# Layer 3's context projections: from layer 1's attention to layer 0's experts

## The chip, the cores and the metric

The kernel runs on one core of a Trainium2 chip. A core has TensorE (PE below; its weight loads are listed as PEld), VectorE (DVE), ScalarE (ACT), GpSimd (POOL) and SyncE (SP), which issues most of the direct DMA transfers; indirect gathers are issued by POOL. The metric is the device time of one execution in microseconds (us), compared by the median of several runs. The profile is one execution, with times counted from the start of its span.

## The reference

The reference is a decoder of four layers on x of shape (8, 256, 256), with a context of shape (8, 120, 192) that no layer changes. Each layer adds an attention, an attention to the context and a feed-forward network, each followed by a layer norm. Cut to what matters here:

```python
# layer 0, feed-forward: 8 experts, every token goes to the best one
expert_idx = jnp.argmax(router_probs, axis=-1)
for e in range(8):
    h = gelu(x_flat @ w1[e] + b1[e], approximate=False)   # 256 -> 1024
    out += where(expert_idx == e, expert_w, 0)[:, None] * (h @ w2[e] + b2[e])

# layer 1, attention to the context: 16 heads of 16
q = x @ w_q + b_q;  k = context @ w_k + b_k;  v = context @ w_v + b_v
out = softmax(q k^T / 4) v @ w_o + b_o

# layer 3, attention to the context: 8 heads of 64
k = context @ Wk      # (8, 120, 192) @ (192, 512)
v = context @ Wv      # (8, 120, 192) @ (192, 512)
```

The last two products hang on nothing that the layers compute, so a kernel may do them at any time before layer 3.

## The kernel before

The stages run in this order: layer 0's attention, its attention to the context (`l0_xattn`, about 206 to 254 us), its experts (`l0_ffn`, about 254 to 512, the end running into the next stage), layer 1's attention (`l1_attn`, to 756), its attention to the context (`l1_xattn`, to about 925), its experts, and the rest. Tokens are held as 16 tiles of 128 (`X`), and turned as `xT`. While a stage runs, the weights of the next one are loaded into the other of two buffers (`load`, L120): a stage's buffer is free for the stage after the next once its last reader is done.

Inside a stage the program names the engine of each operation, and the framework puts the operations of each engine in an order of its own: by place in the program, but what is ready may go ahead of what is not. It also places the semaphores. Once built, each engine's order is fixed. PSUM has eight banks; two belong to transposes (`ps_t`) through the whole kernel, and each stage opens pools for the others.

**Layer 0's experts** (L1016 to L1122) have four parts. Routing: 16 pairs of matmuls give the logits `plog`, then DVE finds the best expert per token (`route`, L891), PE counts places (`pos`, `cnt`), DVE works out the slot of each token, PE finds for each slot its token (`found`, in `takers`, L951), and ACT and DVE make the list `take` of it. Three PSUM banks serve this, then one. The blocks: 23 blocks of 128 slots (L1093 to L1113); each gathers its expert's weights where they differ from those in the buffer (`we`, two buffers), its 128 rows (`xe`), and does 256 to 1024, Gelu on ACT, and back to 256, with four PSUM banks (`ph`, `py`). DVE adds the bias and SP stores the block (`yd`, L1113). The taking back (L1114 to L1122): POOL gathers each token's row of `yd`, DVE scales and adds it and does the norm, PE transposes it into `xT`.

**Layer 1's attention to the context** goes by batches b = 0 to 7 in `attention16` (L640). For each b the program has the scores for the exponentials of b (`exps16`), in two steps, between them the scores of b + 1 that give the largest per row (`largest16`, reduced by DVE at L509), then transposes of these into q (`lower16`, L544, added by DVE at L546), the sums of values (`sums16`, L613), and for even b the projections of the next pair (`project`, L739). What follows a batch (the projection out, the norm, the transposes, the router's logits of the next stage in `choose`, L755) is put into the next batch. All of these take their PSUM banks in turn from one ring of eight (`bank`, L455).

The work that is moved is `context3` (L770). For one batch it projects layer 3's keys (four 128-row parts of two products each) and values (two products 512 wide), has ACT copy the keys (L777) and DVE the values (L782) out of PSUM, and SP store both in DRAM (L778, L783). `inside` (L785) puts it behind the second step of scores of each batch, ahead of `lower16`. The stored values have 65 columns per head, and the last is 1; two buffers (`v3`) get it once from POOL (L736). Layer 3 reads keys and values back at L1758 and L1760, from 1537 us on. The two weights come with layer 1's (L721 to L724) into the buffer that layer 0's experts used for their gate, so they are issued once the last router matmul has read it.

Of the kernel before, what the change touches and what calls it, by code (L numbers as in the profile page):

```python
# [11 lines left out]
F32 = mybir.dt.float32  # L12
# [6 lines left out]
PSUM = bass.MemoryType.PSUM  # L19

P = 128
B, S, D = 8, 256, 256
NT = B * S // P
NTOK = B * S
SC, DC = 120, 192
# [20 lines left out]
class Net:  # L46
# [672 lines left out]
    def load_l1_xattn(self):  # L719

        *w, spare = self.load(  # L721
            *((f"l1x_w{n}", 2) for n in "qkvo"), ("l3x_wk", 2), ("l3x_wv", 2),
            rows=("l1x_bv", "l1x_bo"), spare=16 * NT + 8,
        )  # L724
        top = spare[:, : 16 * NT].rearrange("p (a t k) -> p a t k", a=2, k=8)
        self.top1, self.top1_i, self.w_sums = top[:, 0], top[:, 1].bitcast(U32), spare[:, 16 * NT :]
        return w

    def l1_xattn(self, w):
        nc = self.nc  # L730
        wq, wk, wv, wo, wk3, wv3, bv, bo = w
        with ExitStack() as ctx:
            work, low, vps = self.attn16_pools(ctx, "x1", SC, 1)
            v3 = [work.tile([SC, 8, 65], F32, name=f"v3{n}", bufs=1) for n in range(2)]
            for t in v3:
                nc.gpsimd.memset(t[:, :, 64:], 1.0)  # L736
            bv, bo = self.everywhere(bv, work, "bv"), self.everywhere(bo, work, "bo")

            def project(b, vp):  # L739
                kv = work.tile([P, 2, 2, 2 * SC], F32, name="kv")  # L740
                ctxT = self.ctxT[:, :, b * SC : (b + 2) * SC]
                self.project16(kv, wk, ctxT, self.col("l1x_bk"), 2 * SC, "k")
                qv = work.tile([P, 2, 2, 512], F32, name="qv")
                self.project16(qv, wq, self.xT[:, :, b * S : (b + 2) * S], self.col("l1x_bq"), 512, "q")
                for n in range(2):
                    pv = self.bank([P, 512])[:SC, :D]
                    self.mm(pv, [(ctxT[:, c, n * SC : (n + 1) * SC], wv[:, c, :]) for c in range(2)])
                    self.values16(vp[:, n, 0, :], pv, SC, bv)
                return qv, kv

            zero = work.tile([1, D], F32, name="zero", bufs=1)
            nc.gpsimd.memset(zero, 0.0)
            nc.sync.dma_start(self.xd1[0:1, :], zero)

            def choose(b):  # L755

                xd = self.xd1[1 + b * S : 1 + (b + 1) * S, :].rearrange("(t p) d -> p t d", p=P)
                nc.sync.dma_start(xd, self.X[:, 2 * b : 2 * b + 2, :])
                pl = self.bank([P, 2, 256])[:, :, :32]
                for j in range(2):  # L760
                    i = 2 * b + j
                    self.mm(pl[:, j, :], [(self.xT4[:, c, i, :], self.gate1[:, c, :]) for c in range(2)])
                lg = work.tile([P, 2, 32], F32, name="lg")
                nc.scalar.copy(lg, pl)
                for j in range(2):
                    i = 2 * b + j
                    nc.vector.max(self.top1[:, i, :], lg[:, j, :])
                    nc.vector.max_index(self.top1_i[:, i, :], self.top1[:, i, :], lg[:, j, :])

            def context3(b):  # L770

                ctxT = self.ctxT[:, :, b * SC : (b + 1) * SC]
                pk = self.bank([P, 4, P])[:, :, :SC]
                for m in range(4):
                    self.mm(pk[:, m, :], [(wk3[:, c, m * P : (m + 1) * P], ctxT[:, c, :]) for c in range(2)])
                kT = work.tile([P, 4, SC], F32, name="k3")
                nc.scalar.copy(kT, pk)  # L777
                nc.sync.dma_start(self.k3[b], kT.rearrange("p m s -> p (m s)"))  # L778
                pv = self.bank([P, 512])
                self.mm(pv[:SC], [(ctxT[:, c, :], wv3[:, c, :]) for c in range(2)])  # L780
                v = v3[b % 2]
                nc.vector.tensor_copy(v[:, :, :64], pv[:SC].rearrange("p (h d) -> p h d", d=64))  # L782
                nc.sync.dma_start(self.v3[b], v.rearrange("p h d -> p (h d)"))  # L783

            def inside(b):  # L785
                return lambda: None, lambda: context3(b), lambda: None

            self.attention16(
                project, low, vps, [SC], False, wo, bo, work, then=choose,
                ready=(lambda: None, lambda: None, inside),  # L790
            )

            o = 0
            for j, (_, k, n, _) in enumerate(L2X):
                n *= k // P
# [215 lines left out]


    def load_l0_ffn(self):
        return self.load(("l0f_gate", 2))

    def l0_ffn(self, w):  # L1016
        nc, tc = self.nc, self.tc
        (gate,) = w
        E, FC = 8, 8
        NB = NT + E - 1  # L1020
        with (
            tc.tile_pool(name="f0", bufs=1) as pool,
            tc.tile_pool(name="f0w", bufs=3) as work,
            tc.tile_pool(name="f0d", bufs=1, space=bass.MemoryType.DRAM) as dram,
        ):
            with tc.tile_pool(name="f0r", bufs=1, space=PSUM) as ps:
                plog = ps.tile([P, NT, E], F32, name="plog")
                for i in range(NT):
# [34 lines left out]
            )  # L1063
            with tc.tile_pool(name="f0t", bufs=1, space=PSUM) as ps:
                take = self.takers(block[:, 1], group, 1, pool, work, ps, pool)
            past = pool.tile([P, NB, E], F32, name="past")
            nc.vector.tensor_tensor(
                past,
# [20 lines left out]
            with tc.tile_pool(name="f0p", bufs=2, space=PSUM) as ps:  # L1089
                for turn, n in enumerate(turns):  # L1090
# [20 lines left out]
                    y = work.tile([P, D], F32, name="y")  # L1111
                    nc.vector.tensor_tensor(y, py, b2, ALU.add)  # L1112
                    nc.sync.dma_start(yd[n * P : (n + 1) * P, :], y)  # L1113
                for i in range(0, NT, 2):  # L1114
                    z = work.tile([P, 2, D], F32, name="z")
                    for j in range(2):
# [1260 lines left out]
```

## Time and profile before

| | |
|---|---|
| median of 9 runs | 2445.3 us (2441.64 to 2452.65) |
| profiled execution | 2450.77 us, span 2448.9 us |
| busy share of the span | PE 83%, PEld 61%, DVE 63%, ACT 38%, POOL 28% |
| mean granted clock of PE | 0.90 |
| `l0_xattn`, 206 to 254 us | PE busy 42.1 of 48 us |
| routing, 254 to 293 us | PE busy 22.1 of 39 us, granted clock 0.50 |
| expert blocks, 293 to 492 us | PE busy 183.7 of 199 us |
| taking back until layer 1 starts, 492 to 512 us | PE busy 2.6 of 20 us |
| `l1_attn`, 512 to 756 us | PE busy 223.9 of 244 us |
| `l1_xattn`, 756 to 925 us | PE busy 149.9 of 169 us, DVE 119.2, ACT 69.8 |

A line of the order of time has the start in us, the time in us from start to end, the engine, the line of the program, the operation, what it writes and from what, shapes, and how many were merged; in brackets the idle time of the engine before it and what ended that. Matmuls are pipelined, so their durations overlap, and of a run of them the start of the next line is the better end. A product in float32 is issued as two instructions, so `context3` shows as 16 matmuls of 120 columns and 4 of 512. A window's line has its length, the busy time of each engine in it, the granted clock as a share of full speed, the busy share of the DMA engines and GB/s.

### The profile page before, as it was taken

To read this page: it belongs to the slowest core of one execution; us is meant where nothing else is said; L and a number is where in the kernel's file an instruction comes from. 1 tells how busy PE (TensorE), PEld (TensorE's weight loads), DVE (VectorE), ACT (ScalarE), POOL (GpSimd) and SP (SyncE) were. 2 spreads that over 40 slices of the span, in tenths; PEclk is the share of its full clock that TensorE was granted. 3 is DMA by queue.
4 is the path that set the end of the run, shared out by engine and by line. 5 is a ranking of instruction groups with operands and counts; after the bars stand their busy time and mean duration, and the time that the engine had idled before them with its cause. 6 is when DMAs were issued, how large, how long until landed. Compare 5 with 4: busy or idle time off the path is not lost. (4 is left out here: it accounts for less than half of the span.)

```text
span 2448.9 us, 38544 instructions
## 1 busy us (share of the span) xinstructions
PE 2023.4 (83%) x14051; PEld 1483.5 (61%) x14051; DVE 1545.1 (63%) x5022; ACT 931.0 (38%) x2056; POOL 682.9 (28%) x731
## 2 busy tenths in 40 slices
PE   7998699969998986987779777578898899877895
PEld 4665588835556665863445443466677778665674
DVE  4666300076666766664567688678678877853774
ACT  2332133313333345221334225234554455443662
POOL 1012222031112112544341102344345334520232
PEclk9999699979999996996899888788999999887997
DMA  2000443210002111861110100222222122310000
GB/s 92 2 2 18 164 149 119 74 37 1 2 1 78 48 41 63 255 201 58 35 36 2 65 1 32 85 75 60 69 62 78 49 78 69 114 49 9 1 18 19
DMA packets 69045, 147.54 MB, mean 60 GB/s; under 512 B 15864, under 2 KB 39560, under 8 KB 66928
## 3 DMA queue, kind: packets, MB, share of 16 engines
q0 software_dynamic: 30528, 81.81, 11.0%
q1 hardware_dynamic: 35564, 59.47, 7.3%
q10 hardware_dynamic: 2756, 3.72, 0.4%
q8 instruction: 113, 1.85, 0.3%
q14 instruction: 84, 0.69, 0.1%
HBM read 175.56 MB, written 23.76 MB: 81 GB/s over the span
## 5 line engine op out<-in xcount | busy, mean ns | idle before, releaser
L988 POOL DMA_INDIRECT rows<-in_l2f_table_dram,index x240 | 249.6, 1040 | 259.9 <-PE po L1661 87.3
L144 PE MATMUL ph<-xeT,we 128*128 128x128 f32 (+1 forms) x992 | 175.8, 319 | 19.0 <-DMA we<-in_l0f_experts_dram,wrow 14.1
L144 PE MATMUL pp<-xT,w 128*128 128x256 f32 (+1 forms) x672 | 186.7, 422 | 2.6 <-DVE hT L1135 1.6
L144 PEld LDWEIGHTS ph<-xeT,we 128*128 128x128 f32 x992 | 151.3, 201 | 40.8 <-DMA we<-in_l0f_experts_dram,wrow 15.4
L185 PE MATMUL pt<-ident,X 128*128 128x128 f32 x352 | 75.8, 331 | 117.3 <-DVE X L199 107.0
L600 POOL TENSOR_TENSOR aT<-sides,inv 128x256 f32<-128x256 f32 x64 | 46.6, 728 | 420.9 <-DVE sides L598 327.4
L144 PEld LDWEIGHTS pp<-xT,w 128*128 128x128 f32 x672 | 134.7, 208 | 29.1 <-issue 6.1
L186 ACT COPY xT<-pt 128x512 f32<-128x512 f32 x88 | 51.5, 585 | 256.9 <-PE pt L185 256.8
L185 PEld LDWEIGHTS pt<-ident,X 128*128 128x128 f32 x352 | 47.5, 161 | 154.4 <-DVE X L199 71.2
L988 POOL DMA_INDIRECT xe<-xd,take x87 | 86.3, 992 | 180.1 <-DVE y L1112 75.4
L1661 PE MATMUL po<-rows,diag 128*128 128x256 f32 x480 | 126.3, 403 | 11.5 <-ACT diag L1660 11.4
L1112 DVE TENSOR_TENSOR y<-py,we 128x256 f32<-128x256 f32 x23 | 9.8, 424 | 195.8 <-PE py L144 195.8
L144 PE MATMUL py<-we,hT 128*128 128x256 f32 x496 | 130.1, 387 | 0.2 <-DVE hT L1135 0.2
L564 ACT ACTIVATE e<-sc 128x512 f32<-128x512 f32 (+1 forms) x146 | 77.4, 602 | 100.4 <-PE sc L492 66.9
L1661 PEld LDWEIGHTS po<-rows,diag 128*128 128x128 f32 x480 | 92.1, 200 | 31.8 <-ACT diag L1660 19.0
L1106 ACT ACTIVATE hT<-ph,we 128x128 f32<-128x128 f32 x184 | 65.6, 366 | 117.8 <-PE ph L144 93.4
L1599 DVE SCALAR_TENSOR_TENSOR junk<-rows,X 128x256 f32<-128x256 f32 x224 | 93.8, 419 | 20.6 <-DMA rows<-in_l2f_table_dram,index 18.6
L492 PE MATMUL sc<-kv,qv 32*128 32x128 f32 (+2 forms) x1520 | 103.3, 317 | 3.0 <-ACT e L564 1.9
L144 PE MATMUL sc<-xT,w 128*128 128x512 f32 x216 | 103.4, 628 | 1.4 <-ACT xT L186 1.4
L199 DVE TENSOR_SCALAR X<-z,ln_mv,rs_y 128x256 f32<-128x256 f32 x176 | 66.4, 420 | 58.5 <-POOL rs_y L155 58.2
L492 PEld LDWEIGHTS sc<-kv,qv 32*128 32x128 f32 x1520 | 79.9, 189 | 32.3 <-issue 25.0
L492 PE MATMUL sc<-qv,kv 32*128 32x128 f32 (+2 forms) x1352 | 96.3, 340 | 0.1
(570 smaller groups left out, 5136.4 us busy)
## 6 DMA issues: line engine op xcount, KB each, us to landing
we<-in_l1f_experts_dram SPq DMA_DIRECT2D x32, 384.0 KB
yd<-y SPq DMA_DIRECT2D x32, 256.0 KB
w<-in_l2x_w_dram SPq DMA_DIRECT2D x1, 4096.0 KB
v<-v SPq DMA_DIRECT2D x16, 243.8 KB
rows<-in_l2f_table_dram,index POOLq DMA_INDIRECT x240, 3.2
yd<-y SPq DMA_DIRECT2D x23, 128.0 KB
X<-in_x_dram SPq DMA_DIRECT2D x8, 256.0 KB
xd<-X ACTq DMA_DIRECT2D x8, 256.0 KB
```

What stands on the lines that cost most here:

```text
L144: self.nc.tensor.matmul(out, lhsT=lhsT, rhs=rhs, start=n == 0, stop=n == last and bias is None)
L185: nc.tensor.transpose(pt[:, c, j, :], self.X[:, i0 + j * step, c * P : (c + 1) * P], self.ident)
L186: nc.scalar.copy(self.xT4[:, :, i0 : i0 + step + 1 : step, :], pt)
L199: nc.vector.tensor_scalar(self.X[:, i, :], z[:, j, :], mv[:, j, 0:1], r[:, j : j + 1], ALU.subtract, ALU.mult)
L492: nc.tensor.matmul(sc[: shape[0], part], lhsT=lhsT, rhs=rhs, start=mask is None, stop=True, skip_group_check=True)
L564: lambda r, sc: nc.scalar.activation(e0[m][:n0, r], sc, AF.Exp),
L600: nc.gpsimd.tensor_tensor(out, split(both), split(inv), ALU.mult)
L988: self.nc.gpsimd.indirect_dma_start(out=out, out_offset=None, in_=table, in_offset=bass.IndirectOffsetOnAxis(ap=index, axis=0), **({} if r ...
L1106: nc.scalar.activation(hT[:, g + f, :], ph[:, f, :], AF.Gelu, bias=b1[:, g + f : g + f + 1])
L1112: nc.vector.tensor_tensor(y, py, b2, ALU.add)
L1599: nc.vector.scalar_tensor_tensor(junk, row, 1.0, x, ALU.mult, ALU.mult, accum_out=out)
L1661: nc.tensor.matmul(po, lhsT=diag, rhs=rows[:, k, D:], start=False, stop=(g, k) == (groups[-1][0], size - 1))
```

## The change

`context3` leaves `l1_xattn`, with its `inside`, its `v3` buffers and the two weights. In `l0_ffn` it stands in two places: for batches 0 to 3 behind `takers`, at the end of the routing, and for batches 4 to 7 behind the loop over blocks, ahead of the taking back. It has a PSUM pool of its own of two banks, open through the whole stage (`f0c`), in place of the ring. The copy of the values goes from DVE to ACT. The two weights are loaded with the gate, so the buffer that holds them is free for layer 1's weights only after the last `context3`.

```diff
 def load_l1_xattn(self):
     *w, spare = self.load(
-        *((f"l1x_w{n}", 2) for n in "qkvo"), ("l3x_wk", 2), ("l3x_wv", 2),
-        rows=("l1x_bv", "l1x_bo"), spare=16 * NT + 8,
+        *((f"l1x_w{n}", 2) for n in "qkvo"), rows=("l1x_bv", "l1x_bo"), spare=16 * NT + 8,
     )
 ...
 def l1_xattn(self, w):
-        v3 = [work.tile([SC, 8, 65], F32, name=f"v3{n}", bufs=1) for n in range(2)]
-        for t in v3:
-            nc.gpsimd.memset(t[:, :, 64:], 1.0)
 ...
-        def context3(b):
-            ...
-        def inside(b):
-            return lambda: None, lambda: context3(b), lambda: None
         self.attention16(
             project, low, vps, [SC], False, wo, bo, work, then=choose,
-            ready=(lambda: None, lambda: None, inside),
         )
 ...
 def load_l0_ffn(self):
-    return self.load(("l0f_gate", 2))
+    return self.load(("l0f_gate", 2), ("l3x_wk", 2), ("l3x_wv", 2))

 def l0_ffn(self, w):
+        tc.tile_pool(name="f0c", bufs=2, space=PSUM) as ps3,
 ...
+        v3 = [pool.tile([SC, 8, 65], F32, name=f"v3{n}") for n in range(2)]
+        for t in v3:
+            nc.gpsimd.memset(t[:, :, 64:], 1.0)
+
+        def context3(b):
+            ctxT = self.ctxT[:, :, b * SC : (b + 1) * SC]
+            pk = ps3.tile([P, 4, P], F32, name="c3")[:, :, :SC]
+            for m in range(4):
+                self.mm(pk[:, m, :], [(wk3[:, c, m * P : (m + 1) * P], ctxT[:, c, :]) for c in range(2)])
+            kT = work.tile([P, 4, SC], F32, name="k3", bufs=2)
+            nc.scalar.copy(kT, pk)
+            nc.sync.dma_start(self.k3[b], kT.rearrange("p m s -> p (m s)"))
+            pv = ps3.tile([P, 512], F32, name="c3")
+            self.mm(pv[:SC], [(ctxT[:, c, :], wv3[:, c, :]) for c in range(2)])
+            v = v3[b % 2]
+            nc.scalar.copy(v[:, :, :64], pv[:SC].rearrange("p (h d) -> p h d", d=64))
+            nc.sync.dma_start(self.v3[b], v.rearrange("p h d -> p (h d)"))
 ...
             take = self.takers(block[:, 1], group, 1, pool, work, ps, pool)
+            for b in range(0, B // 2):
+                context3(b)
 ...
                 nc.sync.dma_start(yd[n * P : (n + 1) * P, :], y)
+            for b in range(B // 2, B):
+                context3(b)
             for i in range(0, NT, 2):
```

More of the change, by code (lines that the diff above doesn't have):

```diff
@@ L730, in l1_xattn @@
         nc = self.nc
-        wq, wk, wv, wo, wk3, wv3, bv, bo = w
+        wq, wk, wv, wo, bv, bo = w
         with ExitStack() as ctx:
             work, low, vps = self.attn16_pools(ctx, "x1", SC, 1)
-            v3 = [work.tile([SC, 8, 65], F32, name=f"v3{n}", bufs=1) for n in range(2)]
-            for t in v3:
-                nc.gpsimd.memset(t[:, :, 64:], 1.0)
             bv, bo = self.everywhere(bv, work, "bv"), self.everywhere(bo, work, "bo")
@@ L768, in choose @@
                     nc.vector.max_index(self.top1_i[:, i, :], self.top1[:, i, :], lg[:, j, :])
-            def context3(b):
[L772 to L783, printed above, removed]
-            def inside(b):
-                return lambda: None, lambda: context3(b), lambda: None
             self.attention16(
                 project, low, vps, [SC], False, wo, bo, work, then=choose,
-                ready=(lambda: None, lambda: None, inside),
             )
@@ L1013, in load_l0_ffn @@
     def load_l0_ffn(self):
-        return self.load(("l0f_gate", 2))
+        return self.load(("l0f_gate", 2), ("l3x_wk", 2), ("l3x_wv", 2))
     def l0_ffn(self, w):
         nc, tc = self.nc, self.tc
-        (gate,) = w
+        gate, wk3, wv3 = w
         E, FC = 8, 8
```

## The prediction

> **What bounds the kernel now.** I read the page's busy times first (TensorE, PE below, 83% of the span), then the table of windows by stage, then the order of time on PE in the two stages that the change touches. The chain that ended last is followed back only to 1571 us, so it says nothing about either stage; there I go by what PE waits for. The window table has the columns PE, PE weight load, DVE, ACT, POOL, granted clock, DMA share, GB/s:
>
> ```profile
> core 0: us, PE busy (x) PEld busy (x) DVE busy (x) ACT busy (x) POOL busy (x), PEclk, DMA share, GB/s
> 293.00:492.00 199.00, 183.68 (x1148) 164.88 (x1148) 9.34 (x22) 72.92 (x207) 39.78 (x41) 0.96 0.33 116
> ...
> 756.00:925.00 169.00, 149.91 (x1451) 106.85 (x1450) 119.20 (x314) 69.77 (x137) 29.16 (x42) 0.92 0.16 55
> ```
>
> Layer 1's attention to the context (756 to 925) keeps PE busy for 150 of 169 us, the blocks of layer 0's experts (293 to 492) for 184 of 199. Both are PE's. The routing ahead of the blocks is another thing: PE is full up to 269.5 and then stands still three times, for DVE twice and for the first gather once.
>
> ```profile
> 254.10:269.50 15.40, 14.72 (x70) 14.29 (x69) 1.76 (x10) 1.17 (x2) 1.23 (x3) 0.50 0.39 130
> 269.50:274.70 5.20, 0.27 (x3) 0.20 (x3) 4.55 (x54) 0.57 (x2) 0.00 (x0) 0.50 0.67 234
> ...
> 277.80:283.60 5.80, 0.17 (x2) 0.01 (x1) 5.24 (x30) 0.00 (x0) 1.14 (x1) 0.50 0.00 0
> ...
> 286.70:291.90 5.20, 0.04 (x1) 0.04 (x1) 0.18 (x1) 0.18 (x1) 3.56 (x4) 0.50 1.02 394
> ```
>
> These holes are 5.2 + 5.8 + 5.2 = 16.2 us, all at a granted clock of 0.50. Two more places where PE waits lie behind them: for experts' weights inside the blocks (list of waits of 293 to 492: total, times, longest) and for the first normalized rows after the last block (order of time on PE):
>
> ```profile
> PE ph L144 <- DMA we<-in_l0f_experts_dram,wrow: 14.1, 5, 3.3
> ```
> ```profile
> 507.04 1.13 PE L185 MATMUL pt<-ident,X 128*128 128x128 f32 x4 [14.75 <-DVE X L199]
> ...
> 512.34 4.42 PE L144 MATMUL sc<-xT,w 128*128 128x512 f32 x6 [0.68 <-ACT xT L186]
> ...
> 517.03 2.74 PE L144 MATMUL sc<-xT,w 128*128 128x512 f32 x6
> ```
>
> So the change takes PE work out of a stage that is PE's and puts it beside 16.2, 14.1 and 14.75 us of waiting. The whole question is how much it frees there and how well it fits here.
>
> **What it removes.** One context3 in the order of time of the attention (PE, DVE and ACT together):
>
> ```profile
> 871.96 2.05 PE L144 MATMUL sc<-ctxT,w 128*128 128x120 f32 x16
> ...
> 872.38 0.62 ACT L564 ACTIVATE e<-sc 120x512 f32<-120x512 f32 x1
> ...
> 873.85 1.88 PE L144 MATMUL pt<-w,ctxT 128*120 128x512 f32 x4
> 873.85 2.35 DVE L509 TENSOR_REDUCE low<-sc 128x4 f32<-128x480 f32 x4
> ...
> 876.25 0.55 PE L544 MATMUL pt<-ident,low 128*128 128x128 f32 x3 [0.41 <-DVE low L509]
> ...
> 879.18 1.93 PE L613 MATMUL sc<-e,vp 120*32 120x256 f32 x32
> ...
> 881.05 0.49 PE L492 MATMUL sc<-qv,kv 32*120 32x256 f32 x3
> ```
>
> It holds PE from 871.96 to 875.57, 3.61 us: 8 times that is 28.9 us, the upper end of the gain. But the transposes behind it (L544) still wait 0.41 us for DVE's reductions. Context3 is standing where PE would wait in any case. Taken away alone, it leaves a hole of 876.25 - 871.96 = 4.3 us, and the gain is what moves into it. The sums of values (L613, 1.9 us) can: their last exponentials are ready at 873.00, and they lie behind the hole. Then the next scores start about 1.9 us sooner; qv, which they need, is done at 876.83 + 1.41 = 878.24, no obstacle. For b = 0, 2, 4 the projections of the next pair follow (781.92 to 788.90, 7.0 us) and can fill the rest, so I give those the full 3.6. Gain: 3 x 3.6 + 5 x 1.9 = **20.3 us**. The lower end is below zero. If nothing moves into the hole, the clock may fall: at 916.17 eight matmuls of 128x256 took 3.89 us after a wait of 2.94, where the same eight took 1.99 at 867.80. That is a loss of 1.9 in each of the five batches without projections. DVE loses eight copies of 0.68 and ACT eight of 0.56; neither ends the batch, so nothing for these.
>
> **Contexts 0 to 3, written behind the routing.** They depend on no token, and the trace shows that what is ready is issued ahead of its place in the program (L960 at 256.79, well before L896 at 269.79). So I expect them in the three holes. At full clock four need 14.4 us and fit in 16.2. At half clock, 16 matmuls of 128x128 took 3.57 us (293.02 to 296.59) and the loads before 512-wide ones stood 0.85 us apart (513.36, 514.21, 515.06), so one context needs 3.57 + 3.4 = 7.0, four 28: 11.8 us too much, and PE keeps its order, so routing waits behind. Between 0 and 11.8 I take the middle, **+6**, for the holes are only partly at either clock once work stands in them.
>
> [...] In 254.1 to 269.5 PE was busy 14.72 of 15.40 us and the clock still stood at 0.50. [...]
>
> **Contexts 4 to 7, written behind the blocks.** 14.4 us. Behind the last block they vanish in 14.75 us, beside waits for weights in 14.1; put between a block's own matmuls, where PE has no gap, all 14.4 count, and four pairs of ACT copies (0.56 and about 0.6 for the wider one) ahead of a Gelu that PE waits for add up to 4.8. The order of the new program is not to be seen here: **+7** of 0 to 19.
>
> **The clock.** The first block took 293.02 to 302.92, 9.9 us, the second 7.7 (to 310.66); the first six matmuls of layer 1's attention 4.42 against 2.74. A PE that worked before would save up to 2.2 + 1.7 = 3.9: **-2** of 0 to -3.9.
>
> **What else moves.** SP: 16 store issues of 0.33 us leave the attention, where they pass 8 writes of X, and go in among 23 stores of yd that are spread over 190 us: 0; a pair ahead of the last yd, which the final gathers wait for, costs 0.7. A context store that waits for ACT holds the yd behind it, with three y buffers (two blocks, 15 us) as cover. DMA: four contexts write 4 x 484 KB = 1.9 MB during routing, but the 2 MB of weight loads at 269.8 to 272.5 leave it, since that buffer is now held by the last context: 0. If the first gather (287.43 to 291.87, most of the last hole) had to queue behind them all, 1.9 MB at that hole's 394 GB/s are 5 us. Layer 1's weights then load after the last context and are needed at 756, 240 us later; without that cover some 8 us (DMA was busy with them from 269.8 to about 277.5). Layer 3's two weights ride behind the gate's load at 210, DMA share 0.11: 0. POOL's two memsets (0.11 us) fall into its 25.4 us of idling before 282.46: 0. DVE's copy goes to ACT, which worked 2.3 of 39 us during routing: 0. Two PSUM banks stay taken until the last context; layer 1's attention, which wants six, starts at 512, so 0 unless those contexts end later.
>
> **Sum:** -20.3 + 6 + 7 - 2 = -9.3. The profiled execution took 2450.8 us (span 2448.9), 5.5 above the median of the runs, 2445.3. So 2450.8 - 9.3 = 2441.5, and in terms of the median **2436**.
>
> **Rivals.**
> 1. All of it is hidden. 16.2 + 14.75 + 14.1 us of waiting are more than 28.9. Against it: half clock and PE's fixed order. -20.3 - 3.9 = -24.2: 2421.
> 2. Work only changes its place. The attention gives 12 (between 1.9 and 3.6 for few batches, little for the others), the experts take 11: 2444, no change. A difference under 0.2% (4.9 us) is about what a measurement of this kernel can't tell from none.
> 3. The hole opens (slower). The order on PE stays, sums of values behind L544, and each batch without projections stands still for 4.3 us and then runs slow. Gain 3 x 3.6 - 5 x 1.9 = 1.3, cost 11: +9.7, 2455. It decides as soon as the attention gives less than 11 us. For it speaks the 0.41 us wait behind every context; against it, that in layer 1's own attention, with no such filler, sums of values (599.91 to 603.3) do stand before and around the transposes L544.
> 4. The contexts land between the blocks' matmuls at 14.4 + 4.8 and overrun the routing by 11.8: 31 - 20.3 = +10.7, 2456. Slower once more than 20 of the moved 28.9 us are exposed.
>
> **How the numbers follow.** Forecast (-5 to -16) 0.44; rival 1, 0.08; rival 2, 0.20; rival 3, 0.13; rival 4, 0.15. Faster 0.44 + 0.08 = 0.52, same 0.20, slower 0.28. The likeliest case alone spans 2429 to 2440. For 8 in 10, I leave out the far half of rival 1 and the far half of 3 and 4: 2425 to 2454.
>
> **What would show it.** Right: 756 to 925 shrinks to some 149 us, with L613 ahead of the last L544 in batches without projections; the stretch from the first plog to the first block's start grows from 39 us to about 45; the blocks with the tail grow by some 5. Wrong in the first step: L544 waits 3 us or more for low in each batch, and the granted clock of the attention falls below 0.92. Wrong in the second: contexts stand ahead of the last plog or among pos and found, and DVE's route steps wait for them. Wrong in the third: context matmuls inside blocks that have no wait for weights, or none at all between 254 and 512 with a tail beyond 530.

## The result and the profile after

The changed kernel is slower. Its median is 2463.1 us (18 runs, 2452.1 to 2467.7) against 2447.6 for the kernel before in the same comparison (59 runs); the ratio is 1.0058, with a 95% interval of 1.0049 to 1.0067, so +14.2 us (+12.0 to +16.4). The two medians alone differ by 15.5. The forecast was 2436, or 9.3 us less than before. The profiled execution of the changed kernel has a span of 2459.5 us.

The table of windows, cut at the same events in both traces (first router matmul, first block's first matmul, last block's last matmuls, first projection of the context), shows where the time went. Columns: PE, PE weight load, DVE, ACT, POOL, granted clock, DMA share, GB/s. The kernel before:

```profile
254.14:293.02 38.88, 21.94 (x121) 18.53 (x120) 17.02 (x125) 2.33 (x7) 6.59 (x9) 0.50 0.53 187
293.02:490.40 197.38, 182.08 (x1141) 163.54 (x1142) 9.34 (x22) 72.53 (x206) 39.76 (x41) 0.96 0.33 117
490.40:756.78 266.38, 228.84 (x2110) 137.92 (x2109) 175.37 (x450) 90.77 (x165) 61.42 (x76) 0.95 0.05 15
756.78:925.30 168.52, 149.13 (x1450) 106.55 (x1448) 119.15 (x314) 69.23 (x135) 28.69 (x41) 0.92 0.15 53
```

The changed kernel:

```profile
250.97:296.06 45.09, 41.51 (x252) 34.39 (x252) 17.34 (x125) 9.13 (x19) 6.69 (x11) 0.83 0.51 179
296.06:502.24 206.18, 188.69 (x1171) 167.67 (x1170) 9.34 (x22) 74.62 (x210) 39.77 (x41) 0.95 0.35 122
502.24:767.58 265.34, 228.56 (x2111) 137.63 (x2109) 174.94 (x450) 90.80 (x165) 61.49 (x74) 0.95 0.05 16
767.58:936.42 168.84, 138.81 (x1289) 94.38 (x1287) 114.31 (x306) 64.94 (x127) 28.73 (x41) 0.83 0.08 29
```

Routing grew by 6.2 us, the blocks by 8.8, the taking back with layer 1's attention shrank by 1.0, and layer 1's attention to the context, which lost all of context3, grew by 0.3. With the rest behind it (1523.6 before, 1523.1 after) that is +13.8. The spans differ by only 10.6, since the profiled execution of the changed kernel reached the first router matmul 3.2 us sooner; up to there only the loading of the two weights is new.

So the price was near the forecast and the gain was missing altogether. In the last window PE is busy 10.3 us less (28.9 us of matmuls were taken out), stands still for 30.0 us in place of 19.4, and its clock fell from 0.92 to 0.83. The waits of PE in that window, in the changed kernel (total, times, longest):

```profile
PE pt L185 <- DVE X L199: 10.2, 5, 3.4
PE pt L185 <- DVE low L509: 9.6, 3, 3.4
```

In the kernel before, waits for `low` made 5.2 us there (2.2 + 1.6 + 1.4), and waits of L185 for `X` one of 3.4. The order of time on PE in batch 2 of the changed kernel shows the second row's wait:

```profile
820.77 0.33 PE L544 MATMUL sc<-ident,low 128*128 128x128 f32 x1
824.46 1.12 PE L185 MATMUL pt<-ident,X 128*128 128x128 f32 x4 [3.37 <-DVE low L509]
825.37 0.85 PE L544 MATMUL sc<-ident,low 128*128 128x128 f32 x3
...
827.72 1.75 PE L144 MATMUL sc<-gate,xT 128*128 128x32 f32 x8
829.40 3.64 PE L613 MATMUL sc<-e,vp 120*32 120x256 f32 x32
```

The second row's wait stands in batches 2, 4 and 6. There the sums of values (L613) did not move into the hole: all 32 matmuls are still behind L544, and in 2 and 4 the next pair's projections are behind them. In batch 2 they take 3.64 us, where the same 32 took 1.93 at 879.18 in the kernel before: from 823.01 to 833.25 PE runs at half clock. In batch 0 28 of the 32 do stand ahead of the last transposes, and in batches 1, 3 and 5 twelve, behind a wait of 1.46 us for `X`. Batch 1:

```profile
805.60 1.62 PE L613 MATMUL pt<-e,vp 120*32 120x256 f32 x10
...
809.00 1.06 PE L613 MATMUL sc<-e,vp 120*32 120x256 f32 x2
809.99 0.90 PE L544 MATMUL sc<-ident,low 128*128 128x128 f32 x3
```

What L185 waits for in batch 2 is not `low` itself. It reads `X`, which is ready at 822.70, and writes one of the two banks `pt`, which the ring shares with these transposes. It starts 0.1 us after the first of the two reductions of `pt` has ended (about 824.36):

```profile
822.62 1.22 DVE L509 TENSOR_REDUCE low<-sc 128x4 f32<-128x480 f32 x2
823.75 1.21 DVE L509 TENSOR_REDUCE low<-pt 128x4 f32<-128x480 f32 x2
```

L544 behind it does read `low`, whose last reduction ends at 824.96. Context3 also took two turns of the ring in each batch, so without it the scores fall into other banks. How much of the holes is due to that, no run here shows.

In the routing the contexts (tile `c`) went among everything, and not four of them but six and a half: ahead of the first block's first matmul stand all 20 matmuls of six contexts and 12 of a seventh. The order of time on PE of the changed kernel:

```profile
261.23 0.76 PE L144 MATMUL c<-ctxT,w 128*128 128x120 f32 x2
261.78 1.73 PE L144 MATMUL plog<-w,xT 128*128 128x8 f32 x8
...
267.85 0.95 PE L144 MATMUL plog<-w,xT 128*128 128x8 f32 x8
268.66 1.10 PE L144 MATMUL c<-w,ctxT 128*120 128x512 f32 x2
269.60 1.94 PE L144 MATMUL c<-ctxT,w 128*128 128x120 f32 x16
...
276.67 0.46 PE L144 MATMUL c<-ctxT,w 128*128 128x120 f32 x2
276.97 0.17 PE L900 MATMUL pos<-before,ones_bf 128*128 128x8 bf16 x1
```

They stand ahead of the last logits and between the counts (`pos`) and the finds (`found`), so each step of the routing waits for a piece of context. The clock rose, from 0.50 to 0.83, and one context takes 3.6 us there (269.60 to 273.2). Contexts 4 to 7 did not stay behind the blocks either. Two and a half of them stand in the routing, the rest (28 matmuls) among the blocks, and ACT copied the last of them out at 337.7, in the first quarter of the blocks. The first block took 14.7 us (296.06 to 310.74), against 9.9 before, and not only for the matmuls in it. A copy of values waits there for the store of an earlier one out of the same buffer, the Gelu (L1105) stands behind the copy on ACT, and PE waits for the Gelu:

```profile
300.07 0.60 PE L144 MATMUL py<-we,hT 128*128 128x256 f32 x2
302.39 0.58 ACT L1020 COPY v<-c 120x512 f32<-120x512 f32 x1 [3.66 <-DMA v<-v]
302.87 0.63 ACT L1105 ACTIVATE hT<-ph,we 128x128 f32<-128x128 f32 x2
303.29 1.29 PE L144 MATMUL ph<-xeT,we 128*128 128x128 f32 x8 [2.62 <-ACT hT L1105]
```

The hole behind the last block is still open, 14.76 us against 14.75:

```profile
502.24 1.89 PE L144 MATMUL py<-we,hT 128*128 128x256 f32 x8
518.88 1.14 PE L185 MATMUL pt<-ident,X 128*128 128x128 f32 x4 [14.76 <-DVE X L199]
```

### The profile page after: what moved, and what is told of

The parts are those of the page before. It is cut to its first block, busy times and chain, and to the rows that moved or that the text cites. A ratio compares the mean times of both kernels' runs of the same rounds, so it can differ in the third digit from the quotient of the medians.

```text
span 2459.5 us, 38541 instructions
## 1 busy us (share of the span) xinstructions
PE 2035.9 (83%) x14051; PEld 1490.8 (61%) x14051; DVE 1539.2 (63%) x5014; ACT 935.7 (38%) x2064; POOL 685.8 (28%) x731
## 5 line engine op out<-in xcount | busy, mean ns | idle before, releaser
L185 PE MATMUL pt<-ident,X 128*128 128x128 f32 x352 | 77.0, 333 | 133.5 <-DVE X L199 113.8
L185 PEld LDWEIGHTS pt<-ident,X 128*128 128x128 f32 x352 | 47.6, 161 | 172.6 <-DVE X L199 73.7
L1105 ACT ACTIVATE hT<-ph,we 128x128 f32<-128x128 f32 x184 | 65.5, 367 | 117.2 <-PE ph L144 89.8
L144 PEld LDWEIGHTS py<-we,hT 128*128 128x128 f32 x496 | 88.3, 195 | 11.1 <-DVE hT L1136 3.1
```

The source lines that it names most:

```text
L144: self.nc.tensor.matmul(out, lhsT=lhsT, rhs=rhs, start=n == 0, stop=n == last and bias is None)
L185: nc.tensor.transpose(pt[:, c, j, :], self.X[:, i0 + j * step, c * P : (c + 1) * P], self.ident)
L1105: nc.scalar.activation(hT[:, g + f, :], ph[:, f, :], AF.Gelu, bias=b1[:, g + f : g + f + 1])
```

## The experiments

Theory 1 says that context3 filled waits and kept the clock up, so taking it away frees nothing, and that the order on PE keeps the hole open. Theory 2 says that the removal does free its 20 us and the changed kernel loses some 35 elsewhere. Where a run's attention is given, it is from the first projection of the context to the last router matmul of the stage, as in the tables above.

### The removal alone, and what fills the hole

**Context3 taken out of the attention.**

```diff
...
+            v3 = [work.tile([P, 8, 65], F32, name="v3", bufs=1)]
+            nc.gpsimd.memset(v3[0], 1.0)
...
-                pk = self.bank([P, 4, P])[:, :, :SC]
-                for m in range(4):
-                    self.mm(pk[:, m, :], [(wk3[:, c, m * P : (m + 1) * P], ctxT[:, c, :]) for c in range(2)])
-                kT = work.tile([P, 4, SC], F32, name="k3")
-                nc.scalar.copy(kT, pk)
-                nc.sync.dma_start(self.k3[b], kT.rearrange("p m s -> p (m s)"))
-                pv = self.bank([P, 512])
-                self.mm(pv[:SC], [(ctxT[:, c, :], wv3[:, c, :]) for c in range(2)])
-                v = v3[b % 2]
-                nc.vector.tensor_copy(v[:, :, :64], pv[:SC].rearrange("p (h d) -> p h d", d=64))
+                kT = v3[0].rearrange("p h d -> p (h d)")[:, : 4 * SC]
+                nc.sync.dma_start(self.k3[b], kT)
+                v = v3[0][:SC]
```

> The kernel before, without context3's matmuls and copies in layer 1's attention to the context; a tile of ones is stored in their place, so layer 3's keys and values are left out of what is computed. It is the removal half of the change alone. Theory 1 (filler: the context stood in a wait for DVE's reductions, and without it PE stands there instead and its clock falls): 0 against the kernel before, -3 to +3 us; the attention keeps some 169 us, with PE busy near 139 and a granted clock near 0.83. Theory 2 (the removal does free the 20 us that I forecast, and the changed kernel loses some 35 us in the experts): -17 to -23 us, the attention near 149 us.

Ratio to the kernel before 1.0028 (1.0015 to 1.0040): 2456.5 against 2450.3 us. Removing 28.9 us of matmuls costs 7 us by the ratio. Its window of the attention:

```profile
763.42:937.11 173.69, 142.27 (x1289) 97.09 (x1287) 115.16 (x306) 64.64 (x127) 28.81 (x41) 0.81 0.15 51
```

Against the kernel before, PE stands still 31.4 us in place of 19.4 (+12.0). Its busy time falls from 149.1 to 142.3 instead of to 120.2, so what stayed got 22.0 us slower. 12.0 + 22.0 - 28.9 = +5.1, which is the difference of the two windows (5.2). Theory 2 falls. Theory 1 had said -3 to +3 us, and it is slower than that. The profiled execution is the slowest of the ten (2467.8 us), with 204.0 us in the blocks, whose code is as before, so 5.2 is a high figure for the attention; the sign rests on the ratio.

**The same matmuls, with nobody reading them.**

```diff
                 for m in range(4):
                     self.mm(pk[:, m, :], [(wk3[:, c, m * P : (m + 1) * P], ctxT[:, c, :]) for c in range(2)])
...
-                nc.scalar.copy(kT, pk)
...
                 self.mm(pv[:SC], [(ctxT[:, c, :], wv3[:, c, :]) for c in range(2)])
...
-                nc.vector.tensor_copy(v[:, :, :64], pv[:SC].rearrange("p (h d) -> p h d", d=64))
```

> The kernel before, with context3's matmuls left where they are in the attention, but their banks read by nobody: no copies by ACT and DVE, a tile of ones stored instead (layer 3's keys and values are left out). Against the kernel without context3 (2456.5, attention 173.7 us, granted clock 0.81) it has 28.9 us more of PE's work and nothing else. Theory 1 (the work filled waits and kept the clock up): it is faster than that one by some 6 us, within 2 us of the kernel before, with the attention near 168 us at a clock near 0.92. Theory 2 (the removal is slow for another reason, such as DVE's and ACT's copies or the order of other things): it is as slow as the one without context3 or slower, 2456 to 2485 us.

Ratio 1.0001 (0.9989 to 1.0014): 2450.7 against 2449.8. Theory 1 was right. With 28.9 us more of PE's work than the kernel without context3, it is as fast as the kernel before:

```profile
757.76:926.38 168.62, 149.85 (x1450) 107.53 (x1448) 114.91 (x306) 64.82 (x127) 28.77 (x41) 0.91 0.15 53
```

The copies by DVE and ACT, gone here too, are worth nothing, as I had put them. What counts is context3's work in the hole, together with its two turns in the ring of banks: this run keeps both, the one without context3 has neither, and the two are not separated here.

**Only the keys' half of it.**

```diff
-                pv = self.bank([P, 512])
-                self.mm(pv[:SC], [(ctxT[:, c, :], wv3[:, c, :]) for c in range(2)])
...
-                nc.vector.tensor_copy(v[:, :, :64], pv[:SC].rearrange("p (h d) -> p h d", d=64))
```

> The kernel before with only the keys' 16 matmuls of context3 in each batch (1.9 of 3.6 us); the values' products and copies are left out and ones stored for the values. It asks how PE's time depends on the amount of filling. Between no filler (+7 us, attention 173.7, clock 0.81) and all of it (0, attention 168.5, clock 0.92). If the clock falls with any wait of 2 us and more, it is near the one without: +3 to +7. If half is enough to keep the clock up, the rest of the wait (some 2 us per batch) is all that is left, and it is as fast as before or up to 8 us faster: the wait is then no shorter than 1.9 + 0.4 us, the gain at most 8 x 1.7 = 13.6 us less what stays as a wait. If every us taken away were gained it would be 13.6 us faster.

Ratio 1.0014 (1.0000 to 1.0027), 2452.6 against 2448.7; attention 169.5 us at a clock of 0.90, PE busy 141.4. 13.8 us less work again gave nothing: busy time fell by 7.7, and the wait grew from 19.4 to 28.1. The clock fell little, from 0.92 to 0.90. This lies between no filler and all of it, so it doesn't say with which waits the clock falls.

**Twice the filler.**

```diff
-                return lambda: None, lambda: context3(b), lambda: None
+                return lambda: None, lambda: (context3(b), context3(b)), lambda: None
```

> The kernel before with every context3 of the attention made twice (its results stored twice). It measures what 3.6 us of PE's work cost there once the wait is full. Theory 1: the first context lies in a wait of about its own length and is free, the second has 0.4 us of wait left and costs its 3.6 us each: +24 to +29 us. If the second costs less than 2 us each (under +16), PE has more waiting left there than L544's 0.41 us show, and the gain of a removal is smaller for that reason and not for the order. Theory 2: +20 us too, as a context costs the same whether it is the first or the second.

Ratio 1.0113 (1.0085 to 1.0140): 2480.0 against 2450.3. The attention took 190.7 us, 22.2 more; PE was busy 175.5 us of it, at a clock of 0.95. The first context per batch is free and the second costs 2.8 us of its 3.6 by this trace, a little under theory 1's +24. By the ratio the eight cost 27.7 us, 3.5 each, within it. Theory 2 had priced both contexts alike, at 2.5 us. The run of the removal, not this one, shows the first to be different.

**Sums of values ahead of the transposes.** `sums16` issues its matmuls, then runs `between`, which holds the transposes of the next batch's reductions and the turning of the batch before, and then divides. This is so only in the attention to the context.

```diff
-            self.divided16(aT[:, m, :], av, work)
+            avs.append(av)
+            if not between:
+                self.divided16(aT[:, m, :], av, work)
+        for step in between:
+            step()
+        if between:
+            for m in range(2):
+                self.divided16(aT[:, m, :], avs[m], work)
...
-                self.lower16(q[b + 1], low[(b + 1) % 2])
+                between.append(lambda: self.lower16(q[b + 1], low[(b + 1) % 2]))
...
-                before[1]()
+                between.append(before[1])
```

Without context3:

> The same as the one without context3 (layer 3's keys and values left out), and in the attention to the context each batch's sums of values (L613) are issued ahead of the next batch's transposes of the reductions (L544), the division by the sums behind them. Theory 1: it is the order on PE that keeps the wait open; with 1.9 us of sums in a hole of 3 to 4 us for 7 batches it gives 8 to 15 us against the kernel before, and the granted clock of the attention comes back towards 0.9. Theory 2 (order is no matter, the time was freed already): no more than 2 us from the one without context3.

Ratio 0.9975 (0.9962 to 0.9989), 2445.8 us. That is 6.1 faster than the kernel before, 10.7 faster than the same without the new order. The waits for `X` at L185 fell from 10.2 to one of 3.4, and L544 now waits seven times for `low`, 10.1 us together, 1.8 at most. The attention's window, and one batch on PE:

```profile
756.94:920.46 163.52, 139.80 (x1289) 100.19 (x1288) 113.74 (x306) 63.57 (x127) 28.75 (x41) 0.81 0.16 54
```
```profile
813.72 2.44 PE L614 MATMUL sc<-e,vp 120*32 120x256 f32 x32
816.09 0.33 PE L544 MATMUL sc<-ident,low 128*128 128x128 f32 x1
817.46 0.55 PE L544 MATMUL sc<-ident,low 128*128 128x128 f32 x3 [1.04 <-DVE low L509]
```

The sums (L614 here) stand in the hole, and the wait behind them is 1.0 in place of 3.4. The time of PE without work fell from 31.4 to 23.7. So the order on PE is what held the first part of the gain back. The clock did not come back, against what I had written: still 0.81. So the sums ahead, which I had put at 1.9 us in each of eight batches, 15 in all, are worth 5 us in the attention. The projections, which I had in the hole as well, are still behind L544 here (820.03 in this batch), so the whole of the forecast order was not run.

The same in the changed kernel, with everything computed:

> The changed kernel with the sums of values (L613) issued ahead of the next batch's transposes of the reductions (L544) in the attention to the context; everything is computed. Without context3 this order gave 2456.5 - 2445.8 = 10.7 us. Theory 1: it gives some 8 to 11 us here too, 2463 to about 2453, still some 3 us over the kernel before, since what the contexts cost in the experts (e3: 12 us) stays. Theory 2 (the place in the experts is all that matters): within 3 us of the changed kernel.

Ratio to the kernel before 1.0017 (1.0000 to 1.0035), 2454.4 us; the changed kernel stands at 1.0058. The order takes back some 10 us of 14, as theory 1 said, and the attention is 161.7 us. Some 4 us stay.

The same in the kernel before, context3 in its place:

> The kernel before, context3 in its place, and the sums of values (L613) issued behind context3 and ahead of the next batch's transposes (L544); everything is computed. It is the candidate for a version faster than both. In the kernel before L544 waits only 0.4 us behind a context, some 3 us in seven batches, so the order has that to give at most: -3 to 0 us against the kernel before. If the order gives its 10 us here too, as without context3, it does not work by the wait for the reductions and my account of it is wrong. If it costs 2 us or more, the next batch's scores wait for q behind the sums.

Ratio 1.0007 (0.9995 to 1.0019): no change. The attention shrank by 2.2 us in the trace (166.3, clock 0.92), which the whole does not show. The order helped only where the hole is open (10.7 us without context3). No kernel here that computes everything beats the kernel before.

### The addition alone

**All eight contexts added in the experts, context3 left in the attention.** The new ones are stored to places that nobody reads.

```diff
+        self.k3_2 = dram.tile([B, P, 4 * SC], F32, name="k3_2")
+        self.v3_2 = dram.tile([B, SC, 8 * 65], F32, name="v3_2")
...
                 take = self.takers(block[:, 1], group, 1, pool, work, ps, pool)
+                for b in range(0, B // 2):
+                    context3(b)
...
                     nc.sync.dma_start(yd[n * P : (n + 1) * P, :], y)
+                for b in range(B // 2, B):
+                    context3(b)
```

> The kernel before, with context3 left in the attention and a second copy of all eight contexts in layer 0's experts as in the changed kernel, stored to places that nobody reads. It is the addition half of the change alone. Theory 1: it costs what the two traces show there, 6.2 us from first plog to first block and 8.8 us in the blocks, so +11 to +17 us, with the attention at 169 us. Theory 2: +33 to +38 us.

Ratio 1.0050 (1.0034 to 1.0065), 2462.6 against 2450.3: +12.3 us. In the trace the routing took 45.8 us (+6.9), the blocks 202.3 (+4.9). Theory 1's price, and nowhere near 35.

**Only contexts 0 to 3 added.**

> The kernel before with contexts 0 to 3 added in layer 0's experts behind the routing, as in the changed kernel, stored to places that nobody reads; context3 stays in the attention, and contexts 4 to 7 are not added. It splits e3's 12 us. Theory 1: 6.2 us from the first plog to the first block as in the changed kernel's trace, the blocks as before: +5 to +8. If it is +10 or more, the contexts of the routing cost time in the blocks too, through transfers or the stores; if below +3, most of e3's cost came from contexts 4 to 7.

```diff
                 take = self.takers(block[:, 1], group, 1, pool, work, ps, pool)
+                for b in range(0, B // 2):
+                    context3(b)
```

Ratio 1.0016 (1.0003 to 1.0029): 2454.1 against 2449.8, +4.3, just under what I wrote. In the trace the routing takes 43.2 us (+4.4), at a clock of 0.74; the blocks are as before, 196.3. The other 8 us of the eight contexts come from 4 to 7, some of which stand before the first block and the rest among the first ones.

**Contexts 4 to 7 added where the change's text puts them,** behind the last block. Their PSUM pool opens only once the blocks' pool is closed, so they can't go ahead.

```diff
+            with tc.tile_pool(name="f0c", bufs=4, space=PSUM) as ps3:
+                for b in range(B // 2, B):
+                    context3(b, ps3)
```

> The kernel before with contexts 4 to 7 added behind the last block of layer 0's experts (their banks come free only when the blocks' do), where PE waits 14.75 us for the first normalized rows; stored to places that nobody reads; context3 stays in the attention. Theory 1 (work is free where PE waits for other engines at the end of a stage): 0, from -3 to +2 us; four contexts take 14.4 us there, the clock stays up, and layer 1's first matmuls, 4.42 us in the trace of before, take about 2.7. If it is +4 or more, the hole isn't PE's to give: the copies hold up ACT, or the stores the last rows of the experts.

Ratio 1.0019 (1.0006 to 1.0032), 2455.0 against 2449.8. The hole of 14.75 us was not free:

```profile
484.58 1.89 PE L146 MATMUL py<-we,hT 128*128 128x256 f32 x8
486.99 2.04 PE L146 MATMUL c<-ctxT,w 128*128 128x120 f32 x16 [0.52 <-DVE y L1133]
...
499.36 1.88 PE L146 MATMUL c<-w,ctxT 128*120 128x512 f32 x4
504.31 0.87 PE L187 MATMUL pt<-ident,X 128*128 128x128 f32 x4 [3.07 <-DVE X L201]
508.84 1.22 PE L187 MATMUL pt<-ident,X 128*128 128x128 f32 x4 [3.66 <-DVE X L201]
```

PE is done with the four contexts at 501.2 and waits again. From the last block's last matmuls to the second set of transposes it is 24.3 us; in the kernel before it is 20.1 (490.40 to 510.53). The hole is a wait for gathered rows, and these came later: a gather of `yd` took 3.6 us to land in the median and 5.2 at most, against 2.8 for each before.

**The same four, copied but not stored.**

```diff
-                nc.sync.dma_start(self.k3_2[b], kT.rearrange("p m s -> p (m s)"))
-                nc.sync.dma_start(self.v3_2[b], v.rearrange("p h d -> p (h d)"))
```

> As the one with contexts 4 to 7 added behind the last block (2455.0, 4.7 over the kernel before), but these four are copied out of their banks and not stored. There the first normalized rows reached PE 19.7 us after the last block's matmuls began, against 16.6 before: the gathers of yd took up to 5.2 us to land, against 2.8, while the core moved 243 GB/s from 494 to 507. If the stores of the contexts are what slows the gathers: back to the kernel before, -3 to +2 us, and gathers that land in some 2.8 us. If it is layer 1's weights, which here load at 501 and not during routing, since the last context holds their buffer: +3 to +6 us as with the stores. If it is ACT or PE: +3 to +6, with gathers that land in 2.8.

Ratio 1.0015 (1.0004 to 1.0026), 2451.6 against 2448.7. The gathers land in 2.8 us again in the median (4.6 at most), and the stretch to the second transposes is 20.8 us (485.27 to 506.03). The DMA traffic of the same 13 us in the two, with the stores and without:

```profile
494.00:507.00 13.00, 8.11 (x45) 5.30 (x43) 8.02 (x39) 3.46 (x6) 6.08 (x8) 0.96 0.80 243
```
```profile
494.00:507.00 13.00, 9.78 (x51) 6.28 (x49) 10.83 (x54) 3.46 (x6) 7.60 (x8) 0.95 0.52 156
```

So 3.5 of the 4.1 us at this place are the stores of 484 KB per context beside the gathers. Layer 1's weights, which load from 502 on here, may have the other 0.6. The whole did not come back to zero: +3.0 us by the medians. The trace has 0.6 of it in this place and some 2.4 behind it: from the last block's last matmuls to the first product with the causal mask in layer 1 it is 53.7 us, against 50.6. There DVE waits 2.72 us for a gather (at 509.60), while the core moves 219 GB/s from 505 to 515, against 72 in the same stretch before. That points to layer 1's weights; no run takes them away alone.

### The changed kernel without the contexts' work

```diff
+            v3 = pool.tile([P, 8, 65], F32, name="v3")
+            nc.gpsimd.memset(v3, 1.0)
...
             def context3(b):
...
+                nc.sync.dma_start(self.k3[b], v3.rearrange("p h d -> p (h d)")[:, : 4 * SC])
+                nc.sync.dma_start(self.v3[b], v3[:SC].rearrange("p h d -> p (h d)"))
```

> The changed kernel without the matmuls and copies of the contexts in layer 0's experts; a tile of ones is stored in their place early in that stage (layer 3's keys and values are left out). The attention is the changed kernel's, and its two weights and 16 stores are not there either, which the run without context3 still had. It says what the removal alone does to the rest of the program: against the changed kernel it takes away what the contexts cost in the experts (e3: 12 us), against the kernel before it adds the removal. Theory 1: slower than the kernel before by 0 to 7 us (2449 to 2456 by this set's runs of it), routing 39 us, blocks 197 to 200, attention 168 to 174 us at a clock of 0.81 to 0.83. Theory 2 (the removal gains its 20 us once its stores and weights are gone too): 2429, attention near 149.

Ratio 1.0024 (1.0002 to 1.0046). In this set both kernels took some 100 us longer than elsewhere, and this run's trace has that behind 925 us, so only the ratio and the stages before that are used. Routing 38.7 us, blocks 198.5, attention 168.8 at a clock of 0.84, PE busy 138.6: the changed kernel's attention exactly, and the experts of the kernel before. With its stores and its two weights gone as well, the removal still frees nothing. Whether it costs 0 or 7 us differs between the two forms; the windows say 0.3 and 5.2, the ratios +0.24% and +0.28%, and both intervals hold 4 to 9 us. The windows of one execution do not settle it: in the five traces that leave this stage alone it takes 166.8 to 170.1 us.

## Why the prediction was wrong

- **What it removes: wrong, and this is the step that failed.** I gave 20.3 us. It broke at "the gain is what moves into it": I moved all sums of values into the hole in every batch, and behind batches 0, 2 and 4 the projections too. In the new program nearly all sums moved only in batch 0. In 2, 4 and 6 they and the projections stay behind L544 and PE waits 2.9 to 3.4 us; in 1, 3 and 5 twelve of 32 matmuls moved. Measured: 0.3 us lost in the changed kernel's window, 20.6 off. I had the lower end ("below zero") and the row for it, and then took a value far above the middle. The 0.41 us wait behind every context was the evidence, and I weighed it less than the order of another stage.
- **And with the sums ahead it would not have been what I counted.** Eight times 1.9 is 15 us; it is 5.0 us in the attention (168.5 to 163.5). What the projections would add is not shown. I counted 3.6 and 1.9 us per batch as if PE's remaining work kept its speed, while the clock fell to 0.81. I had the row for that too (eight matmuls in 3.89 us after a wait, against 1.99) and used it only for the lower end.
- **Rival 3 was right in its mechanism, and near in its price of the attention partly by luck:** it had +1.3 of gain against 0.3 of loss. But it filled the hole in batches 0, 2 and 4 and opened it in the others, and the widest holes are in 2, 4 and 6. It ended at +9.7 by the costs that I had taken, 6 + 7 - 2; these came out at 14, and its condition, an attention that gives less than 11 us, was met.
- **Contexts 0 to 3 in the routing, +6: it grew by 6.2 in the changed kernel, but with six and a half contexts in it, so that the two agree is luck; these four alone cost 4.4.** The place was not the three holes: they went among logits, counts and finds as well. The two ends of this term, full clock and the row at 0.50, were 11.8 us apart; the granted clock became 0.83, nearer to the full one: 0.50 up to 266.64 and 1.00 from there to the first block. It rose 5.4 us after the first product 120 columns wide (261.23); before, with products of 8 columns alone, it had stood at 0.50 through 15.4 us in which PE was busy for 14.7.
- **Contexts 4 to 7, +7: within its range.** The blocks grew by 8.8 in one pair of traces and by 4.9 with the addition alone. I had left open whether they land in the hole behind the blocks; they landed in the routing and among the first blocks. I had counted ACT's copies ahead of a Gelu with their own 0.56 to 0.6 us; the one that cost time waited 3.66 us for a store, and PE 2.62 behind it. The idea that behind the last block "they vanish in 14.75 us" was wrong: forced there, they cost 4.1 us in that place, through the transfers.
- **The clock, -2: nothing of it came.** The first block, which was to get up to 2.2 us shorter, got 4.8 longer; with contexts 0 to 3 alone it took 9.4 us against 9.9. The other part hung on contexts behind the last block, and where they were forced there, layer 1's first six matmuls took 5.49 us (with the stores) and 5.15 (without) in place of 4.42.
- **DMA, 0: right for layer 1's weights, the yd queue and the first gather (which PE waits 2.98 us for in place of 5.19), wrong for the contexts' own stores.** In the changed kernel a buffer of values that was still being stored held up ACT and PE (the 2.62 us above), and in the tail the gathers took 3.6 us in the median beside the stores, in place of 2.8, where I had counted PE, ACT and 0.7 us for a pair of stores ahead of the last yd.
- **The range** of 2425 to 2454 was cut in the far half of rivals 3 and 4. Measured from my median the time is 2445.3 x 1.0058 = 2459.5. The costs at 14 in place of 11, with rival 3, lead there.

## What to carry to other kernels

Before work is taken out of a busy engine, look at what stands behind it in that engine's fixed order: if the next instruction waits a few tenths of a us for another engine every time (0.41 here), the work may be filling a wait that taking it out turns into idle time (here 28.9 us of matmuls went, and PE stood still 12.0 us longer). Here a filler was free only up to about the length of the wait (the first context of a batch was free, and a second one cost 2.8 us of its 3.6), and on PE the work that stayed ran slower when the waits opened (clock 0.81 and 0.83, in place of 0.92). The gain from removing a filler must be priced with an order that is seen and not one that could be. A hole that waits for transfers was not free for work that brings transfers of its own: 14.2 us of contexts in 14.75 us of waiting cost 4.1 us there, and 0.6 without their stores.

## What the runs showed that I had not expected

**The clock fell after a wait of 1.84 us, and for 10.2.** In the kernel without context3 and with the sums ahead, the longest wait in this stretch is 1.84 us (at 834.7). In steps of 4 us, with the granted clock third from the end:

```profile
833.00:837.00 4.00, 2.16 (x29) 1.19 (x22) 3.52 (x7) 0.33 (x1) 0.44 (x1) 1.00 0.19 66
837.00:841.00 4.00, 3.60 (x31) 2.84 (x30) 3.14 (x14) 1.16 (x3) 0.33 (x1) 0.83 0.00 0
841.00:845.00 4.00, 2.82 (x38) 2.34 (x30) 1.82 (x6) 2.42 (x5) 1.12 (x2) 0.50 0.02 4
845.00:849.00 4.00, 4.00 (x14) 2.70 (x16) 2.24 (x5) 0.00 (x0) 0.00 (x0) 0.50 0.00 0
849.00:853.00 4.00, 4.00 (x78) 2.87 (x79) 2.61 (x8) 2.06 (x4) 2.16 (x3) 0.89 0.00 0
```

The clock halves at 839.65, 3.1 us after the wait has ended, although PE is at work for 3.60 of those 4 us, and comes back 10.2 us later. The wait alone is not shown to be the cause: in the kernel before, the clock fell at 802.26, and in the 3.4 us ahead of that PE was busy for 2.28 us and waited 0.68 us at most, with products only 32 columns wide in between.

**Beside the same wait the clock was low for 10.24 us once and for 3.41 the next time.** In the kernel without context3 the wait of 3.36 us comes in two batches with the same instructions around it:

```profile
823.58 1.11 PE L185 MATMUL pt<-ident,X 128*128 128x128 f32 x4 [3.36 <-DVE low L509]
...
828.51 3.64 PE L613 MATMUL sc<-e,vp 120*32 120x256 f32 x32
...
863.19 1.11 PE L185 MATMUL pt<-ident,X 128*128 128x128 f32 x4 [3.36 <-DVE low L509]
...
867.45 1.93 PE L613 MATMUL sc<-e,vp 120*32 120x256 f32 x32
```

The sums behind it took 3.64 us and 1.93. The granted clock in steps of 0.2 us shows why:

```profile
822.20:822.40 0.20, 0.00 (x0) 0.00 (x0) 0.20 (x2) 0.00 (x0) 0.00 (x0) 0.67 0.14 41
832.40:832.60 0.20, 0.20 (x2) 0.19 (x2) 0.20 (x1) 0.00 (x0) 0.06 (x1) 0.73 0.00 0
863.20:863.40 0.20, 0.20 (x1) 0.20 (x2) 0.20 (x1) 0.00 (x0) 0.00 (x0) 0.57 0.01 0
866.60:866.80 0.20, 0.20 (x5) 0.20 (x3) 0.00 (x0) 0.00 (x0) 0.00 (x0) 0.90 0.00 0
```

These are the steps in which it changes, and the share tells where: it fell at 822.27 and rose at 832.51, fell at 863.23 and rose at 866.64. So it was low for 10.24 us and for 3.41. These two, and the 30.72 us between them, are whole multiples of 3.41 us, and so are all distances between two changes of the clock in this stage in the traces of the kernel before (3.41 to 95.57 us) and of the changed kernel (3.41 to 23.89). Why the same wait came with a longer stretch at half clock the first time, no run shows. Stages that no edit touched differ between traces as well, for reasons that no run tests: in nine traces that leave the blocks alone they took from 194.5 us at a clock of 0.97 to 204.0 at 0.92, and layer 1's attention with the taking back took 271.1 at 0.93 in one run, against 266.4 at 0.95 in the kernel before. A difference of 5 us in one window of one profiled execution is therefore not yet an effect.
